# Small one-hots for the lists, row tiles in groups of four, and adj.T blocks gathered beside the scan: a change to a sparse two-layer graph kernel

## The chip, the core and the metric

The kernel runs on one core of a Trainium2 chip. The metric is the device time of one execution in microseconds (us); a kernel's time is the median of its timed runs. A ratio is always that of a kernel to the kernel before, measured on the same chip in the same rounds: the mean time of its runs over the mean of the other's. It is therefore not quite the ratio of the medians that I quote. Brackets after a ratio are its 95% interval.

Profiled times (starts of instructions, stages) come from one execution of each kernel.

## The reference, cut to what matters

Two layers, each preceded by a LayerNorm and a ReLU, and each with a residual. `x` is 4096 x 512, `adj` is 4096 x 4096 and sparse, with denser rows and columns at low indices.

```python
h = jnp.maximum(_layernorm(x), 0.0)
x = x + L0(h, adj, W)      # mx = h @ W, scaled by a tanh/artanh of norms;
                           # gamma from the row's square; A @ (gamma - 1), A @ (gamma * X), sum of A's rows;
                           # midpoint, relu, more tanh/artanh scalings
h = jnp.maximum(_layernorm(x), 0.0)
x = x + L1(h, adj, ...)    # node softmax(h @ node_w) * edge softmax where adj > 0, then adj * att @ (h @ weight)
```

## The kernel before

The kernel never multiplies by the whole of `adj`. For each of 32 row tiles (128 rows of `adj`) it finds which columns have any entry in that tile, packs them into a list, and gathers only those. Three stages matter.

**Stage A, for eight groups of four row tiles.** It loads adj.T in 64 pieces of 1 MB by the sync queue, reduces each piece to "which adj.T row has an entry in which row tile" (the scan), computes each entry's place in the list with small vector operations, and inverts that into a list by matmuls of one-hots (rows of zeros with a single one, which marks an entry's place). Beside it runs phase A: LayerNorm, `h @ W`, and the row `Y` with its extra columns, written to DRAM.

**Stage B.** For each row tile it gathers the listed blocks of adj.T (128 columns each, `at`) and the listed rows of Y (`yg`), multiplies them on TensorE, then does the midpoint and phase C (the projections of the second layer).

**Stage D.** Attention on gathered rows of `h`. The change leaves it alone.

```python
def gather_at(r):                       # adj.T blocks of one row tile
    n = CAPS[r]                         # 6 to 22, 256 in all
    wide = n > WIDE
    t = atp.tile([P, CAPM if wide else WIDE, P], F32, tag=f"at{wide}", bufs=2 if wide else 3)
    for k in range(n):
        nc.gpsimd.indirect_dma_start(out=t[:, k, :], in_=adj_rows, ...)
    nc.sync.dma_start(at_dram[r], t[:, :n, :])      # kept for a later stage
    at_sb[r] = t

def scan_loads(g):
    for b in range(NT // SC):
        s = ap.tile([P, SC, T4 * P], F32, tag="scan", bufs=3)
        nc.sync.dma_start(s, adj_t[...])             # the same sync queue
...
def make_list(r, lo, hi):
    nc.vector.tensor_tensor(oh, lo[:, q, :].unsqueeze(2).to_broadcast([P, NT, P]),
                            iota_h..., ALU.is_equal)  # 4096 elements a partition
    ...                                              # ov: 32 x n, compare and multiply
    for c in range(NT):
        nc.tensor.matmul(ps[:, :n], oh[:, c, :], ov[:, c, :], ...)
...
for g in range(NG):                                  # stage A
    a = [phase_a(2 * g), phase_a(2 * g + 1)]         # two row tiles each
    ...
    for r in range(g * T4, min(g * T4 + T4, AHEAD)): # AHEAD = 3: only the first three tiles
        gather_at(r)
...
for t in range(T4):                                  # stage B
    if r + AHEAD < NT:
        gather_at(r + AHEAD)
    acc = products(r)                                # gathers Y rows, multiplies with at_sb[r]
```

Of the kernel before, what the change touches and what calls it, by code (L numbers as in the profile page):

```python
# [27 lines left out]
F32 = mybir.dt.float32  # L28
F16 = mybir.dt.float16
# [9 lines left out]
P = 128  # L39
# [83 lines left out]
def listed_path(ctx, tc, x, adj_t, w0, weight, bias, node_w, edge_w, out, flag):  # L123
# [11 lines left out]
    YW = D + 2  # L135
    HALF = D // 2
# [18 lines left out]
    iota_i = const.tile([P, P], I32, tag="iotai", name="iotai")  # L155
    nc.gpsimd.iota(iota_i, [[1, P]], base=0, channel_multiplier=0)
    iota_h = const.tile([P, P], F16, tag="iotah", name="iotah")
    nc.vector.tensor_copy(iota_h, iota_i)
# [3 lines left out]
    nc.vector.tensor_copy(part_f, part_i)  # L162
    above_b = const.tile([P, P], BF16, tag="aboveb", name="aboveb")
    nc.vector.tensor_scalar(above_b, iota_h, part_f, None, ALU.is_gt)
# [6 lines left out]
    col_i = const.tile([P, NT], I32, tag="coli", name="coli")  # L171
    nc.gpsimd.iota(col_i, [[P, NT]], base=-(N // 2), channel_multiplier=1)
    col_h = const.tile([P, NT], F16, tag="colh", name="colh")
    nc.vector.tensor_copy(col_h, col_i)

# [4 lines left out]
    count = const.tile([P, NT], F32, tag="count", name="count")  # L180
    idx_y = const.tile([P, sum(CAPS)], I32, tag="idxy", name="idxy")
# [12 lines left out]
    atp = early.enter_context(tc.tile_pool(name="atp", bufs=1))  # L194
# [14 lines left out]
    def layernorm(pool, tag, xs, T, bufs):  # L209

        st = small.tile([P, T, nc.vector.BN_STATS_DIM], F32, tag=f"st{T}", name="st")
        mv = small.tile([P, T, nc.vector.BN_AGGR_DIM], F32, tag=f"mv{T}", name="mv")
        for t in range(T):
            nc.vector.bn_stats(st[:, t, :], xs[:, t, :])
            nc.vector.bn_aggr(mv[:, t, :], st[:, t, :])
        ve = S.tile("ve", T)
        nc.vector.tensor_scalar(ve, mv[:, :, 1], LN_EPS, None, ALU.add)
        rstd = S.recip(S.sqrt(ve, T), T, "rstd")
        z = pool.tile([P, T, D], F32, tag=tag, name="z", bufs=bufs)
        for t in range(T):  # L220
            nc.vector.tensor_scalar(  # L221
                z[:, t, :], xs[:, t, :], mv[:, t, 0:1], rstd[:, t : t + 1], ALU.subtract, ALU.mult
            )
        return z

    def relu_transposed(pool, z, T, bufs):

        hT = pool.tile([P, DC, T * P], F32, tag="hT", name="hT", bufs=bufs)
        for c in range(DC):
            tp = bank("tp", 2)  # L230
            for t in range(T):
                nc.tensor.transpose(tp[:, t * P : (t + 1) * P], z[:, t, c * P : (c + 1) * P], ident)  # L232
            nc.scalar.activation(hT[:, c, :], tp[:, : T * P], AF.Relu)
        return hT

    at_sb = {}

    def gather_at(r):

        n = CAPS[r]  # L240
        wide = n > WIDE
        t = atp.tile([P, CAPM if wide else WIDE, P], F32, tag=f"at{wide}", name="at", bufs=2 if wide else 3)
        for k in range(n):
            nc.gpsimd.indirect_dma_start(  # L244
                out=t[:, k, :],
                out_offset=None,
                in_=adj_rows,
                in_offset=bass.IndirectOffsetOnAxis(ap=idx_a[:, first[r] + k : first[r] + k + 1], axis=0),
            )
        nc.sync.dma_start(at_dram[r], t[:, :n, :])  # L250
        at_sb[r] = t

    AHEAD = 3


    with tc.tile_pool(name="a", bufs=1) as ap:

# [35 lines left out]
        def places(g, f, ps):  # L293
# [21 lines left out]
            nc.vector.tensor_scalar(lo_i, pos, P - 1, None, ALU.bitwise_and)  # L315
            hi_i = ap.tile(shape, I32, tag="hii", name="hii", bufs=2)
            nc.vector.tensor_scalar(hi_i, pos, 7, None, ALU.logical_shift_right)
# [6 lines left out]
        def make_list(r, lo, hi):  # L324

            n, q = CAPS[r], r % T4
            oh = ap.tile([P, NT, P], F16, tag="oh", name="oh", bufs=1)
            shape = [P, NT, P]
            nc.vector.tensor_tensor(  # L329
                oh,  # L330
                lo[:, q, :].unsqueeze(2).to_broadcast(shape),
                iota_h.unsqueeze(1).to_broadcast(shape),
                ALU.is_equal,
            )
            ov = ap.tile([P, NT, CAPM], F16, tag="ov", name="ov", bufs=2)
            shape = [P, NT, n]
            ov = ov[:, :, :n]
            nc.vector.tensor_tensor(
                ov,
                hi[:, q, :].unsqueeze(2).to_broadcast(shape),  # L340
                iota_h[:, :n].unsqueeze(1).to_broadcast(shape),
                ALU.is_equal,
            )
            nc.vector.tensor_mul(ov, ov, col_h.unsqueeze(2).to_broadcast(shape))
            ps = bank("sm", 2)
            for c in range(NT):
                nc.tensor.matmul(ps[:, :n], oh[:, c, :], ov[:, c, :], start=(c == 0), stop=(c == NT - 1))  # L347
            iy = idx_y[:, first[r] : first[r] + n]
            nc.vector.tensor_scalar(iy, ps[:, :n], float(N // 2), None, ALU.add)
            nc.vector.tensor_scalar(  # L350
                idx_a[:, first[r] : first[r] + n], ps[:, :n], float(NT), float(N // 2 * NT + r), ALU.mult, ALU.add
            )

        def phase_a(g):
            xs = x_sb[g * T2 // T4][:, g * T2 % T4 : g * T2 % T4 + T2, :]
            z = layernorm(ap, "z", xs, T2, 1)
            hss = S.tile("hss", T2)
            for t in range(T2):
                junk = ap.tile([P, D], F32, tag="junk", name="junk", bufs=2)
                nc.vector.scalar_tensor_tensor(  # L360
                    junk, z[:, t, :], 0.0, z[:, t, :], ALU.max, ALU.mult, accum_out=hss[:, t : t + 1]
                )
            hT = relu_transposed(ap, z, T2, 2)
            yield
            mss = S.tile("mss", T2)
            Y = ap.tile([P, T2, YW], F32, tag="Y", name="Y", bufs=2)
            ym = [bank("mm", 4) for _ in range(T2)]
            for t in range(T2):
                for c in range(DC):
                    nc.tensor.matmul(  # L370
                        ym[t], hT[:, c, t * P : (t + 1) * P], w0_sb[:, c, :], start=(c == 0), stop=(c == DC - 1)
                    )
                junk = ap.tile([P, D], F32, tag="junk", name="junk", bufs=2)
                nc.scalar.activation(junk, ym[t], AF.Square, accum_out=mss[:, t : t + 1])
            yield
            xn = S.norm(hss, T2)
            at = S.artanh_clipped(xn, T2)
            mn = S.norm(mss, T2)
            arg = S.mul(S.mul(mn, S.recip(xn, T2), T2), at, T2, "arg")
            th = S.tanh(arg, T2)  # L380
            s = S.mul(th, S.recip(mn, T2), T2, "s")
            alive = S.tile("alive", T2)
            nc.vector.tensor_scalar(alive, mss, EPS * EPS, None, ALU.is_gt)
            s = S.mul(s, alive, T2, "sl")

            xss = S.mul(S.mul(mss, s, T2), s, T2)
            gam = S.tile("gam", T2)
            nc.vector.tensor_scalar(gam, xss, -1.0, 1.0, ALU.mult, ALU.add)
            nc.vector.reciprocal(gam, gam)
            gm = S.tile("gm", T2)  # L390
            nc.vector.tensor_scalar(gm, gam, 2.0, 1e-15, ALU.mult, ALU.max)
            sg = S.mul(s, gm, T2, "sg")
            nc.vector.tensor_scalar(Y[:, :, HALF], gm, -1.0, None, ALU.add)
            nc.gpsimd.memset(Y[:, :, YW - 1], 1.0)  # L394
            for t in range(T2):
                nc.scalar.activation(Y[:, t, 0:HALF], ym[t][:, 0:HALF], AF.Copy, scale=sg[:, t : t + 1])
                nc.scalar.activation(Y[:, t, HALF + 1 : D + 1], ym[t][:, HALF:D], AF.Copy, scale=sg[:, t : t + 1])  # L397
            nc.scalar.dma_start(y_dram[g * T2 * P : (g + 1) * T2 * P, :].rearrange("(t p) d -> p t d", p=P), Y)
            yield

        for g in range(NG):
            a = [phase_a(2 * g), phase_a(2 * g + 1)]
            tiles = scan_loads(g)
            next(a[0])
            next(a[1])
            f, ps = scan_flags(g, tiles)
            next(a[0])
            next(a[1])
            lo, hi = places(g, f, ps)
            for q in range(T4):  # L410
                make_list(g * T4 + q, lo, hi)
                if q % 2:
                    next(a[q // 2])
            for r in range(g * T4, min(g * T4 + T4, AHEAD)):
                gather_at(r)
# [16 lines left out]
    def products(r):  # L432

        n = CAPS[r]
        acc = [bank("mm", 4) for _ in range(2)]
        for k in range(n):
# [7 lines left out]
            for h in range(2):  # L444
                nc.tensor.matmul(  # L445
                    acc[h][:, 0 : HALF + 1],
                    at_sb[r][:, k, :],
# [4 lines left out]
        at_sb.pop(r)  # L452
# [58 lines left out]
    def phase_c(g):  # L511
        z = layernorm(bp, "zt", x_sb[g], T4, 3)
        for t in range(T4):
# [3 lines left out]
                junk, z[:, t, :], 0.0, nw, ALU.max, ALU.mult, accum_out=logit[:, r : r + 1]  # L517
            )
        yield
        hT = relu_transposed(bp, z, T4, 1)  # L520
# [30 lines left out]
    for g in range(NG):  # L551
        tm = bp.tile([P, T4, D], F32, tag="zt", name="tm", bufs=3)
        da = small.tile([P, T4, 2], F32, tag="da", name="da")
        for t in range(T4):
            r = g * T4 + t
            if r + AHEAD < NT:
                gather_at(r + AHEAD)
# [653 lines left out]
```

## Time and profile before

The time before was 1924.02 us, the median of 3 runs (1923.54 to 1924.39).

I mark the stages by three starts that any profile shows: the first gather of a Y row (end of A), the first gather of an h row (end of B), and the end of the span. The first profile of this kernel was taken of an execution longer than the timed runs.

| profile of the kernel before | A, to the first Y gather | B, to the first h gather | rest | span |
|---|---|---|---|---|
| first | 545.9 | 748.6 | 705.7 | 2000.2 |
| taken again | 528.3 | 679.8 | 714.2 | 1922.3 |

These are two groups of the first profile. The columns are line, engine, operation, output and inputs, count; busy us in all and mean ns of one; idle time of the engine just before them, with what ended most of it.

```profile
L244 POOL DMA_INDIRECT at<-in_adj_t_dram,idxa x256 | 271.1, 1059 | 180.9 <-DVE idxa L350 92.5
L438 POOL DMA_INDIRECT yg<-y,idxy x256 | 249.4, 974 | 210.0 <-PE mm L445 97.2
```

The reader should see that GpSimd issues 512 gathers for A and B at about 1 us each. Its long idle time is no loss where something else is the bound: before the adj.T gathers 92.5 us of it are waits for lists, and before the Y gathers 97.2 are waits for TensorE to free a buffer.

### The profile page before, as it was taken

The numbers are of one execution on the slowest core, as the hardware profiler recorded it, in microseconds if no ns is written. First come the engines' busy times: TensorE is split into PE (matmuls) and PEld (weight loads), VectorE is DVE, ScalarE is ACT, GpSimd is POOL, SyncE is SP. The second block draws the span as 40 slices with busy tenths as digits, with TensorE's granted clock in tenths as the row PEclk, the third lists the DMA queues.
The fourth block names the chain that finished last, engine by engine and source line by source line (L and its number), as shares of the span: only waits on it lengthen the run. The fifth ranks groups of instructions, "written<-read, shape, count | busy, mean of one in ns | idle before, by whom it ended". The sixth has DMA issues, their size and how long they took to land. (4 is left out here: it accounts for less than half of the span.)

```text
span 2000.2 us, 18396 instructions
## 1 busy us (share of the span) xinstructions
PE 1383.7 (69%) x5872; PEld 804.4 (40%) x5872; DVE 851.8 (43%) x2794; ACT 521.9 (26%) x1053; POOL 805.6 (40%) x828
## 2 busy tenths in 40 slices
PE   0422444433385468776787898679999999998988
PEld 0211222221153245443454554345555455555554
DVE  5836999999700325242433455212122222222222
ACT  0211333323200213131331434123232232222222
POOL 0375000000066766675756661144444344444330
PEclk9766766655698679887887999889999999999999
DMA  9564555544265566664656663386887787777761
GB/s 364 169 152 128 187 190 189 188 150 145 80 191 158 134 176 180 186 194 125 206 158 189 199 189 139 116 324 230 277 271 258 267 270 287 252 255 270 260 234 55
DMA packets 146361, 399.56 MB, mean 200 GB/s; under 512 B 17488, under 2 KB 17488, under 8 KB 146000
## 3 DMA queue, kind: packets, MB, share of 16 engines
q0 software_dynamic: 65536, 218.42, 36.2%
q1 hardware_dynamic: 70416, 159.66, 22.1%
q10 hardware_dynamic: 10304, 20.22, 2.8%
q8 instruction: 49, 0.80, 0.2%
q14 instruction: 56, 0.46, 0.1%
HBM read 331.09 MB, written 67.14 MB: 199 GB/s over the span
## 5 line engine op out<-in xcount | busy, mean ns | idle before, releaser
L607 POOL DMA_INDIRECT h<-h,idxy x256 | 241.0, 942 | 345.6 <-PE sm L684 236.0
L445 PE MATMUL mm<-yg,at 128*128 128x257 f32 x1024 | 283.1, 429 | 129.1 <-DMA yg<-y,idxy 97.3
L244 POOL DMA_INDIRECT at<-in_adj_t_dram,idxa x256 | 271.1, 1059 | 180.9 <-DVE idxa L350 92.5
L438 POOL DMA_INDIRECT yg<-y,idxy x256 | 249.4, 974 | 210.0 <-PE mm L445 97.2
L445 PEld LDWEIGHTS mm<-yg,at 128*128 128x128 f32 x1024 | 207.1, 211 | 197.3 <-DMA yg<-y,idxy 133.2
L684 PE MATMUL sm<-h,wT 128*128 128x512 f32 x512 | 270.0, 629 | 6.1 <-DVE zt L699 4.9
L527 PE MATMUL mm<-w,hT 128*128 128x512 f32 x512 | 242.9, 625 | 28.5 <-issue 22.2
L619 ACT COPY kT<-tp 128x512 f32<-128x512 f32 x256 | 144.8, 582 | 367.5 <-PE tp L618 343.0
L634 PE MATMUL mm<-kT,q 128*128 128x512 f32 (+3 forms) x608 | 237.2, 532 | 3.6 <-ACT kT L619 2.0
L641 DVE TENSOR_SCALAR_CACHE_REDUCE e<-mm 128x512 f32<-128x512 f32 (+2 forms) x76 | 45.9, 606 | 319.9 <-PE mm L638 307.0
L275 DVE TENSOR_REDUCE mx<-scan 128x16 f32<-128x2048 f32 x64 | 145.7, 2279 | 63.2 <-issue 33.8
L618 PE MATMUL tp<-ident,h 128*128 128x128 f32 x1024 | 151.8, 279 | 22.9 <-DMA h<-h,idxy 20.7
L618 PEld LDWEIGHTS tp<-ident,h 128*128 128x128 f32 x1024 | 123.3, 143 | 98.7 <-issue 85.8
L527 PEld LDWEIGHTS mm<-w,hT 128*128 128x128 f32 x512 | 100.1, 201 | 144.4 <-issue 133.8
L347 PE MATMUL sm<-ov,oh 128*128 128x6 f16 (+8 forms) x1024 | 32.3, 169 | 174.3 <-DVE oh L329 110.9
L634 PEld LDWEIGHTS mm<-kT,q 128*128 128x128 f32 x608 | 110.2, 191 | 101.3 <-issue 77.6
L370 PE MATMUL mm<-w,hT 128*128 128x512 f32 x256 | 135.0, 676 | 9.9 <-ACT Y L397 9.9
L329 DVE TENSOR_TENSOR oh<-lo,iotah 128x4096 f16<-128x4096 f16 x32 | 141.3, 4417 | 0.0
L232 PE MATMUL tp<-ident,z 128*128 128x128 f32 x256 | 54.5, 352 | 103.3 <-DVE z L221 67.9
L394 POOL MEMSET Y<- 128x2 f32 x16 | 1.7, 106 | 294.3 <-DMA y<-Y 135.6
L561 DVE COPY da<-mm 128x1 f32<-128x1 f32 x64 | 9.7, 156 | 257.9 <-ACT tm L560 181.8
L684 PEld LDWEIGHTS sm<-h,wT 128*128 128x128 f32 x512 | 84.3, 196 | 48.8 <-issue 31.9
(164 smaller groups left out, 1382.4 us busy)
## 6 DMA issues: line engine op xcount, KB each, us to landing
scan<-in_adj_t_dram SPq DMA_DIRECT2D x64, 1024.0 KB
h<-h SPq DMA_DIRECT2D x32, 512.0 KB
y<-Y ACTq DMA_DIRECT2D x16, 514.0 KB
x<-in_x_dram ACTq DMA_DIRECT2D x8, 1024.0 KB
x<-x SPq DMA_DIRECT2D x8, 1024.0 KB
hhT<-hhT SPq DMA_DIRECT2D x32, 256.0 KB
q<-hhT SPq DMA_DIRECT2D x32, 256.0 KB
x<-x SPq DMA_DIRECT2D x32, 256.0 KB
```

The source lines that it names most:

```text
L244: nc.gpsimd.indirect_dma_start(out=t[:, k, :], out_offset=None, in_=adj_rows, in_offset=bass.IndirectOffsetOnAxis(ap=idx_a[:, first[r] + k ...
L275: nc.vector.tensor_reduce(mx[:, :, b * SC : (b + 1) * SC].rearrange("p r c -> p c r"), s.rearrange("p c (r i) -> p c r i", i=P), AX.X, ALU ...
L329: nc.vector.tensor_tensor(oh, lo[:, q, :].unsqueeze(2).to_broadcast(shape), iota_h.unsqueeze(1).to_broadcast(shape), ALU.is_equal,)
L370: nc.tensor.matmul(ym[t], hT[:, c, t * P : (t + 1) * P], w0_sb[:, c, :], start=(c == 0), stop=(c == DC - 1))
L438: nc.gpsimd.indirect_dma_start(out=y, out_offset=None, in_=y_dram, in_offset=bass.IndirectOffsetOnAxis(ap=idx_y[:, first[r] + k : first[r] ...
L445: nc.tensor.matmul(acc[h][:, 0 : HALF + 1], at_sb[r][:, k, :], y[:, h * (HALF + 1) : (h + 1) * (HALF + 1)], start=(k == 0), stop=(k == n - 1),
L527: nc.tensor.matmul(ps, hT[:, c, t * P : (t + 1) * P], w[:, c, :], start=(c == 0), stop=(c == DC - 1))
L607: nc.gpsimd.indirect_dma_start(out=h, out_offset=None, in_=h_dram, in_offset=bass.IndirectOffsetOnAxis(ap=idx_y[:, first[r] + k : first[r] ...
L618: nc.tensor.transpose(tp[:, c * P : (c + 1) * P], h[:, c * P : (c + 1) * P], ident)
L619: nc.scalar.copy(s["kT"][k // KG][:, :, k % KG * P : (k % KG + 1) * P], tp.rearrange("p (c j) -> p c j", c=DC))
L634: nc.tensor.matmul(ps[:, :w], s["q"][:, c * P : (c + 1) * P], kT[:, c, :w], start=(c == 0), stop=False)
L684: nc.tensor.matmul(s["acc"], s["w"][:, k % KG * P : (k % KG + 1) * P], s["h"].pop(k)[:, D : 2 * D], start=(k == 0), stop=(k == n - 1),)
```

## The change

Its intent has three parts.

(a) **Small one-hots.** A place in the list is split at 32 instead of 128 (`QB = 32`), so `oh` has 1024 elements a partition in place of 4096, laid out with NT innermost. `ov` becomes four times as wide. All lists of a group share one PSUM bank and are read out together.

(b) **Groups of four.** Phase A works on four row tiles at a time, and LayerNorm's output, ReLU and the sum of squares move from VectorE to ScalarE.

(c) **Early gathers.** All 256 adj.T blocks are gathered in stage A, beside the scan, stored in DRAM, and read back in stage B by plain DMAs of the sync queue.

```diff
-        oh = ap.tile([P, NT, P], F16, tag="oh", name="oh", bufs=1)
-        nc.vector.tensor_tensor(oh, lo[:, q, :].unsqueeze(2).to_broadcast(shape),
-                                iota_h.unsqueeze(1).to_broadcast(shape), ALU.is_equal)
+        oh = ap.tile([P, QB, NT], F16, tag="oh", name="oh", bufs=2)
+        nc.vector.tensor_tensor(oh, lo[:, j, :].unsqueeze(1).to_broadcast([P, QB, NT]), lo_of, ALU.is_equal)
   ... (ov, the matmuls and the read-out likewise, one PSUM bank for four lists)
-        z = layernorm(ap, "z", xs, T2, 1)
+        h = relu_layernorm(ap, "z", x_sb[g], T4, 1)          # ReLU and scaling on ScalarE
-                nc.vector.scalar_tensor_tensor(junk, z[:, t, :], 0.0, z[:, t, :], ALU.max, ALU.mult, accum_out=...)
+                nc.scalar.activation(junk, h[:, t, :], AF.Square, accum_out=hss[:, t : t + 1])
   ...
 def gather_at(r):
-    t = atp.tile([P, CAPM if wide else WIDE, P], F32, tag=f"at{wide}", name="at", bufs=2 if wide else 3)
+    t = ap.tile([P, CAPM if wide else WIDE, P], F32, tag=f"at{wide}", name="at", bufs=1 if wide else 3)
     for k in range(n):
         nc.gpsimd.indirect_dma_start(...)
     nc.sync.dma_start(at_dram[r], t[:, :n, :])
-    at_sb[r] = t
   ...
-            for r in range(g * T4, min(g * T4 + T4, AHEAD)):
+            for r in range(g * T4, g * T4 + T4):
                 gather_at(r)
   ...
 def products(r):
+    at = bp.tile([P, CAPM if wide else WIDE, P], F32, tag=f"at{wide}", name="at", bufs=1 if wide else 3)
+    nc.sync.dma_start(at[:, :n, :], at_dram[r])
   ...
-            if r + AHEAD < NT:
-                gather_at(r + AHEAD)
             acc = products(r)
```

In the new kernel the adj.T gathers are line 257, their stores line 263, the scan loads line 269, the scan's reduces line 282, the one-hots lines 339 to 345, the list matmuls line 348, the index writes line 357, the Y gathers line 443 and the products line 450.

## The prediction

> **What bounds the kernel now.** I read the engine tenths over the span first, then the groups of instructions, then the windows of the stage that the diff edits, then the waits and the timeline inside it. One proviso: the profiled execution spans 2000.2 us, the timed median is 1924.02, so my us are profiled ones, some 4% long.
>
> The engine tenths (40 slices of 50 us) show three stages.
>
> ```profile
> PE   0422444433385468776787898679999999998988
> ...
> DVE  5836999999700325242433455212122222222222
> ...
> POOL 0375000000066766675756661144444344444330
> ```
>
> The digits say that from 100 to 545 us (stage A: scan of adj.T, lists, first matmul, Y) VectorE is full while GpSimd is idle; from 545 to 1290 (stage B: weighted sums and phase C) GpSimd is at six or seven tenths and TensorE at seven or eight; after 1290 (stage D, attention) TensorE is full. The diff leaves D alone.
>
> Windows of equal kind in stage A (columns: window, its length, then busy us with counts of PE, PEld, DVE, ACT, POOL, then granted clock, DMA share, GB/s):
>
> ```profile
> 287.00:343.00 56.00, 23.38 (x178) 12.73 (x178) 54.03 (x149) 17.65 (x41) 0.20 (x2) 0.63 0.50 176
> 343.00:400.00 57.00, 22.53 (x178) 12.47 (x178) 54.96 (x152) 19.02 (x41) 0.20 (x2) 0.67 0.48 166
> ```
>
> One group of four row tiles takes about 56 us, of which VectorE works 54 to 55. The groups of instructions say on what:
>
> ```profile
> L275 DVE TENSOR_REDUCE mx<-scan 128x16 f32<-128x2048 f32 x64 | 145.7, 2279 | 63.2 <-issue 33.8 <-DMA scan<-in_adj_t_dram 29.2
> ...
> L329 DVE TENSOR_TENSOR oh<-lo,iotah 128x4096 f16<-128x4096 f16 x32 | 141.3, 4417 | 0.0
> ```
>
> The scan costs as much as the one-hots. Also real: the 33.8 us idle, at 113 to 147 us. The sync queue's timeline shows the stores of gathered blocks at 121 and the next scan loads only at 140.6, so loads stood behind stores that waited for gathers.
>
> In stage B one GpSimd instruction goes out every 1.25 us (0.94 us and 0.30 us before it) over long stretches:
>
> ```profile
> 892.98 0.94 POOL L244 DMA_INDIRECT at<-in_adj_t_dram,idxa  x1 [0.30 <-issue]
> 894.23 0.95 POOL L244 DMA_INDIRECT at<-in_adj_t_dram,idxa  x1 [0.30 <-issue]
> 895.48 0.94 POOL L244 DMA_INDIRECT at<-in_adj_t_dram,idxa  x1 [0.30 <-issue]
> 896.72 0.95 POOL L438 DMA_INDIRECT yg<-y,idxy  x1 [0.30 <-issue]
> ```
>
> Gathers of adj.T blocks and of Y rows share that one issuer, and the waits of TensorE in the groups name the Y rows (L445: 97.3 us in all). GpSimd issue and TensorE in turn bound B.
>
> **What the Trainium skill says.** "VectorE: DVE Perf Modes", section "The perf-mode tier table": 16-bit tensor_tensor in SBUF can run at 2 results a cycle, fp32 at one. "Vector Engine (DVE) Microarchitecture Reference", section "5.1 Performance modes": that needs an innermost step of 1 on every operand. The old one-hot reads `lo` with an innermost broadcast: 4417 ns for 4096 elements, with a fixed 150 ns, is 1.04 ns an element, one a cycle; the trace agrees. The new layout has NT innermost everywhere, so I expect two; no instruction of the trace before shows that. "SBUF — State Buffer", section "Practical consequences": GpSimd and some VectorE instructions exclude each other on a shared port, and tensor_reduce never contends. The trace agrees in part: an adj.T gather beside a one-hot lasted 5.05 us in place of 0.94, beside reduces 0.94; the page says tensor_tensor contends with reads only, the trace shows it holding up a gather.
>
> **The change part by part.** Back-to-back VectorE instructions start about 0.07 us apart beyond their streaming time (timeline), so I cost each as elements plus 0.07.
>
> VectorE in A, in all:
> - One-hot `oh`: 4096 to 1024 elements. Was 32 x 4.34 = 139 us. At two a cycle 0.53 + 0.07 = 0.60, x32 = 19. Saves 120.
> - `ov`, compare and multiply: elements rise four-fold, from 32 x 256 to 32,768 a pass. Was 2 x (8.5 + 2.2) = 21; becomes 2 x (17.1 + 2.2) = 39. Costs 18.
> - LayerNorm output and sum of squares to ScalarE: 18 + 23 saved; ScalarE gets 32 x (0.6 + 0.8) = 45 us, minus half its small instructions and table loads. At 18 us of 56 it has room.
> - Groups of four row tiles: the instruction order shows VectorE at 1207 instructions before the first sum, 814 after; some 330 of the 393 gone are tiny, x 0.07 = 23 saved.
> Sum: 441 busy before (windows 0 to 546), minus 120, plus 18, minus 41, minus 23 = 275. That is 34 us a group.
>
> So VectorE stops being A's bound. GpSimd now gathers all 256 blocks in A: 256 x 1.25 = 320 us, and it can't start before the first list, at about 78 us as before (79 us now). That gives 398 us. Additions: VectorE holding the port (short instructions now, say 0.05 us a gather, 13), memsets of Y in GpSimd's order, waits for buffers (one wide, three narrow), stores and scan loads in one sync queue (the built order has scan loads alternating with stores that wait for gathers). I take 35 us for all. A's last gather at about 433, first product at 445; it was 548 (GpSimd's first Y gather at 545.9). Gain 100.
>
> DMA in that stretch: 16.8 MB gathered and 16.8 MB stored move beside 56 MB of scan. From 78 to 113 us gathers alone took 0.31 of the DMA time for about 27 gathers, so 0.4 us of all engines each, 102 in all; the other 87 MB at the 364 GB/s of the first slice take 240. 342 of some 360 us: nearly full, which is why I don't take the 398.
>
> Stage B: 208 adj.T gathers x 1.25 = 260 us leave GpSimd, which keeps 256 x 1.25 = 320. The blocks come back by the sync queue (16.8 MB more read). With operands at hand seven blocks took 6.25 us on TensorE, 0.89 each; sixteen matmuls of phase C took 7.03. Until 622 us no adj.T gather ran, so group 0 (59 blocks at 1.43, the rate with eight Y buffers) stays 84 us. Middle: 197 x 0.89 = 175, plus 384 x 0.44 = 169, plus transposes 40 = 384, plus some 60 of waits on ScalarE that the trace has now ("issue" and "remote" rows). Tail as now, 77. Sum 605 against 742 (548 to 1290): 137, of which I count 115, because TensorE may not fill so well.
>
> Total: 100 + 115 = 215 profiled, about 200 in timed runs. 1924 - 200 = 1724; I say 1725.
>
> **Rivals.**
> 1. DMA or the sync queue becomes A's bound. For it: 342 us of DMA work above; the 33.8 us wait, once before, can now recur for each group; where gathers and scan overlapped (147 to 172 us) VectorE worked only 9.17 of 25 us. Against: the scheduler lets scan loads run over a group ahead. Then A gains 20 to 40 and the time is about 1790.
> 2. B doesn't speed up, since Y gathers (eight in flight, 1.43 us each at 184 GB/s) and ScalarE's slow stretches pace it. For it: from 700 to 1200 TensorE waited only 45 us for Y rows, some 60 for others. Against: GpSimd's unbroken stretches. Then B gains 50: about 1790.
> 3. `ov` and `oh` run at one a cycle. VectorE then needs 275 + 17 + 34 = 326 us, 41 a group, about GpSimd's pace: costs 10 to 20 us.
> 4. More than expected: without gaps TensorE's granted clock (0.84 in mid-B, 1.00 in D) rises and B takes 540: about 1660.
>
> **Range and chances.** Rivals 1 and 2 together give about 1850, rival 4 about 1650. Range 1640 to 1815. To miss 2% both gains must fail, for which only rival 1 at its worst, starving VectorE in every group, is a way: faster 0.94, same 0.04, slower 0.02.
>
> **What would show it.** Right: `oh` near 0.68 us and no GpSimd idle in A; its last adj.T gather near 430 us; first Y gather near 440; no adj.T gather in B; TensorE in mid-B over 0.85 busy; D still about 700 us. Wrong: VectorE idle waiting for scan loads, sync-queue stores waiting for gathers, gathers well over 1 us, or a first product after 490; in B, TensorE waiting as long for Y rows as before, or for reloaded blocks.

## The result, and the profile after

The changed kernel took 1820.95 us (median of 4, 1818.66 to 1821.51) against 1923.88 (1923.54 to 1924.39): ratio 0.9463 [0.9446, 0.9479]. It is faster by 103 us. I had said 1725, with a range of 1640 to 1815: the direction was right, the gain was half of what I had summed, and the time lies just outside the range.

The engine tenths of the kernel after (40 slices of 45 us each):

```profile
PE   0671534555717879999999975899999998898988
...
DVE  5863476556400236444564530122222222222222
...
POOL 1067653355666755445443204344444443344330
```

Stage A is the first twelve digits. VectorE is no longer full there, which is what (a) and (b) were for. But nothing else is full either: GpSimd, which should have become the bound, runs at three to seven tenths. From slice 13 on (stage B) TensorE is at seven to nine, up to the passage to stage D (slices 24 and 25).

The end of A is the first start in the view of the Y gathers (count; shortest, median and longest in ns; first and last start):

```profile
L443 POOL DMA_INDIRECT yg<-y,idxy x256: 940/946/1408, 531.6 to 1010.7; - x128
```

The groups of instructions, after:

```profile
L257 POOL DMA_INDIRECT at<-in_adj_t_dram,idxa x256 | 248.6, 971 | 266.1 <-DVE ml L113 91.0
L443 POOL DMA_INDIRECT yg<-y,idxy x256 | 252.9, 988 | 234.1 <-PE mm L450 178.4
L450 PE MATMUL mm<-yg,at 128*128 128x257 f32 x1024 | 246.9, 394 | 74.1 <-DMA yg<-y,idxy 65.6
...
L282 DVE TENSOR_REDUCE mx<-scan 128x16 f32<-128x2048 f32 x64 | 145.9, 2281 | 112.6 <-DMA scan<-in_adj_t_dram 112.6
```

In B, GpSimd now mostly waits for TensorE to free a Y buffer (178.4 us, against 97.2 in the first profile of before and 40.8 in the second), and TensorE's wait for Y rows is 65.6 us (97.3 and 113.7 before): the stage has passed to TensorE. In A, VectorE waited 112.6 us for scan tiles, against 63.2 us of idle time before those reduces in the first profile of before, and 70.4 in the second. GpSimd was idle 266.1 us before the adj.T gathers; 91.0 of these are the wait for the first list.

What holds up the scan loads stands in the waits of the sync queue in stage A (0 to 500 us; columns: waiting line, what it waited for, us in all, times, longest):

```profile
SPq L263 <- DMA at<-in_adj_t_dram,idxa: 274.7, 71, 22.1
```

The queue spent 274.7 us waiting for gathers to land, so that it could start their stores; 214.0 of these fell before its last scan load went out at 433 us, and only they can hold up loads. Its timeline, in one group's stretch (start, length, what was issued):

```profile
213.84 0.32 SPq L263 DMA_DIRECT2D at<-at  x1
214.27 0.38 SPq L269 DMA_DIRECT2D scan<-in_adj_t_dram  x1
224.65 0.32 SPq L263 DMA_DIRECT2D at<-at  x1
225.08 22.88 SPq L269 DMA_DIRECT2D scan<-in_adj_t_dram  x7
```

Here one scan load goes out right behind each store, and the stores come about 11 us apart (213.84 and 224.65, and one before at 202.25), which is the time of nine gathers, one row tile. With the group's last store gone at 224.65, seven loads follow within 23 us, with no store between them. VectorE's timeline over the same stretch shows what that does to the scan (the bracket is idle time before the instruction and what ended it):

```profile
222.31 2.29 DVE L282 TENSOR_REDUCE mx<-scan 128x16 f32<-128x2048 f32 x1 [8.45 <-DMA scan<-in_adj_t_dram]
...
241.74 0.19 DVE L357 SCALAR_TENSOR_TENSOR idxa<-idxy,tileof 128x32 int32<-128x32 int32 x1
```

VectorE stood idle for 8.45 us before that tile (and for 7.97 and 3.76 us before the ones beside it), and the group's index write came only at 241.74. GpSimd's timeline shows the circle close:

```profile
221.06 0.94 POOL L257 DMA_INDIRECT at<-in_adj_t_dram,idxa  x1 [0.30 <-issue]
222.00 0.12 POOL L400 MEMSET Y<- 128x1 f32 x1
242.20 0.94 POOL L257 DMA_INDIRECT at<-in_adj_t_dram,idxa  x1 [20.08 <-DVE rstd L118]
```

GpSimd ran out of lists at 222.12 us. The next list's indices were written at 241.74, and its gathers began 20 us late, at 242.20. (The releaser that the row names, `rstd`, is another VectorE instruction; releasers are inferred, and it is the index write that ends at 241.93, just before.) This happened five times in A: 22.6, 20.1, 22.8, 22.3 and 13.2 us, 101.0 us together.

Where the time went, by stage, in profiled us:

| | A | B | rest | span |
|---|---|---|---|---|
| before, taken again | 528.3 | 679.8 | 714.2 | 1922.3 |
| after | 531.6 | 567.0 | 718.3 | 1816.9 |
| gain | -3.3 | 112.8 | -4.1 | 105.4 |

The whole gain lies in B. A, in which I had counted on 100 us, gained nothing.

### The profile page after: what moved, and what is told of

Same layout as the page of the kernel before. It is cut to its first block, busy times and chain, and to the rows that moved or that the text cites. A ratio compares the mean times of both kernels' runs of the same rounds, so it can differ in the third digit from the quotient of the medians. Undisturbed runs are those within 1.5% of the kernel's fastest.

```text
span 1816.9 us, 18260 instructions
## 1 busy us (share of the span) xinstructions
PE 1375.9 (76%) x5872; PEld 827.6 (46%) x5872; DVE 689.1 (38%) x2345; ACT 560.0 (31%) x1092; POOL 793.2 (44%) x878
## 5 line engine op out<-in xcount | busy, mean ns | idle before, releaser
L257 POOL DMA_INDIRECT at<-in_adj_t_dram,idxa x256 | 248.6, 971 | 266.1 <-DVE ml L113 91.0
L443 POOL DMA_INDIRECT yg<-y,idxy x256 | 252.9, 988 | 234.1 <-PE mm L450 178.4
L450 PE MATMUL mm<-yg,at 128*128 128x257 f32 x1024 | 246.9, 394 | 74.1 <-DMA yg<-y,idxy 65.6
L450 PEld LDWEIGHTS mm<-yg,at 128*128 128x128 f32 x1024 | 193.9, 195 | 121.5 <-issue 51.2
L531 PE MATMUL mm<-w,hT 128*128 128x512 f32 x512 | 227.9, 596 | 0.0
L282 DVE TENSOR_REDUCE mx<-scan 128x16 f32<-128x2048 f32 x64 | 145.9, 2281 | 112.6 <-DMA scan<-in_adj_t_dram 112.6
L232 PE MATMUL tp<-ident,h 128*128 128x128 f32 x256 | 60.7, 370 | 157.6 <-ACT h L221 135.1
L620 PE MATMUL tp<-ident,h 128*128 128x128 f32 x1024 | 153.7, 281 | 21.8 <-DVE mask L632 14.4
L620 PEld LDWEIGHTS tp<-ident,h 128*128 128x128 f32 x1024 | 125.0, 145 | 97.9 <-issue 86.2
L531 PEld LDWEIGHTS mm<-w,hT 128*128 128x128 f32 x512 | 95.6, 191 | 104.1 <-issue 100.0
L374 PE MATMUL mm<-w,hT 128*128 128x512 f32 x256 | 128.0, 656 | 8.5 <-ACT Y L402 5.0
L232 PEld LDWEIGHTS tp<-ident,h 128*128 128x128 f32 x256 | 38.7, 185 | 187.9 <-ACT h L221 136.9
L348 PE MATMUL sm<-ov,oh 128*32 128x24 f16 (+8 forms) x1024 | 68.6, 230 | 59.9 <-DVE ov L345 59.9
L348 PEld LDWEIGHTS <-oh 128*32 128x32 f16 x1024 | 66.7, 146 | 66.6 <-DVE oh L339 45.8
L663 ACT ACTIVATE e<-e,rmax 128x512 f32<-128x512 f32 (+2 forms) x76 | 49.5, 652 | 146.9 <-DVE rmax L658 146.9
```

The source lines that it names most:

```text
L257: nc.gpsimd.indirect_dma_start(out=t[:, k, :], out_offset=None, in_=adj_rows, in_offset=bass.IndirectOffsetOnAxis(ap=idx_a[:, first[r] + k ...
L282: nc.vector.tensor_reduce(mx[:, :, b * SC : (b + 1) * SC].rearrange("p r c -> p c r"), s.rearrange("p c (r i) -> p c r i", i=P), AX.X, ALU ...
L348: nc.tensor.matmul(ps[:QB, o : o + m], oh[:, :, c], ov[:, :, c], start=(c == 0), stop=(c == NT - 1))
L374: nc.tensor.matmul(ym[t], hT[:, c, t * P : (t + 1) * P], w0_sb[:, c, :], start=(c == 0), stop=(c == DC - 1))
L443: nc.gpsimd.indirect_dma_start(out=y, out_offset=None, in_=y_dram, in_offset=bass.IndirectOffsetOnAxis(ap=idx_y[:, first[r] + k : first[r] ...
L450: nc.tensor.matmul(acc[h][:, 0 : HALF + 1], at[:, k, :], y[:, h * (HALF + 1) : (h + 1) * (HALF + 1)], start=(k == 0), stop=(k == n - 1),)
```

## The experiments

My theory: the stores of gathered blocks wait, in the sync queue, for gathers; scan loads stand behind them; so the lists come late; so the gathers come late, which delays the next stores. The rival that I took most seriously: the DMA engines are full in A, with up to 33.6 MB more moved beside the scan (16.8 gathered and 16.8 stored), and the order in a queue is a symptom. Others: ScalarE or the small steps of phase A hold VectorE up, or my figure for A before was wrong because its profile was of a long execution. Each expectation names the theories that it tells apart.

The changed kernel was not run again beside the experiments. Where I say that a run is so many us faster than the change, I compare medians of different rounds, and the kernel before itself had medians from 1920.16 to 1926.96 us in them. By the ratios, times 1924, the gains over the change are 15 us for gather_late, 36 for store_pool, 60 for store_no_wait, 15 for memset_dve, 58 for store_pool_memset and 64 for store_lag_memset: a few us apart from those of the medians, and the same in kind.

### before_again: the kernel before, unchanged

No edit. It asks whether the 2000.2 us of the first profile belong to the kernel.

> The kernel before, unchanged, profiled a second time: the trace that the prediction rests on spans 2000.2 us although the timed median is 1924. Theory 1 (that one profiled execution lost some 76 us in stage B, in the rows named issue and remote): span near 1924, first Y gather still near 546 us, first h gather of stage D near 1220 instead of 1294. Theory 2 (every profiled execution of this kernel is long): span near 2000 again.

It took 1924.14 us (one look), with a span of 1922.3. The view of its Y gathers gives the end of A:

```profile
L438 POOL DMA_INDIRECT yg<-y,idxy x256: 940/946/1456, 528.3 to 1120.0; - x128
```

So the first profile was of one long execution, by 78 us: 17.6 more in A, 68.8 more in B, 8.5 less in the rest. Everything that the prediction reads from B of the first profile is inflated by that. What made that one execution long stays open.

### gather_late: parts (a) and (b) alone

Based on the kernel after, with the gathers put back into B. Some buffers had to become single for the room (the scan's small tiles, `junk`, and two `Y` instead of three).

```diff
-            for r in range(g * T4, g * T4 + T4):
+            for r in range(g * T4, min(g * T4 + T4, AHEAD)):
                 gather_at(r)
   ...
-        nc.sync.dma_start(at[:, :n, :], at_dram[r])
-                    at[:, k, :],
+                    at_sb[r][:, k, :],
   ...
+            if r + AHEAD < NT:
+                gather_at(r + AHEAD)
             acc = products(r)
```

> The changed kernel with its third part undone: adj.T blocks are gathered in stage B three tiles ahead and used from SBUF, as before; small one-hots and groups of four stay (a few small stage-A buffers single, to fit). Theory 1 (stores that wait for gathers hold up the scan loads in the sync queue, and that alone kept stage A long): without them VectorE paces A at 35 to 42 us a group, first Y gather at 400 to 430 us, B as in the kernel before, time 1790 to 1830. Theory 2 (A is held by the lists, the DMA rate of the scan or the groups of four themselves): first Y gather at 500 or later, time 1880 to 1920.

It took 1806.73 us (1802.08 to 1814.79), ratio 0.9384 [0.9347, 0.9421]. That is faster than the whole change. This is the Y gather's row by its source line (count; shortest, median and longest in ns; first and last start):

```profile
L447 POOL DMA_INDIRECT yg<-y,idxy x256: 942/949/1412, 410.0 to 998.4; - x128
```

A ends at 410.0, so (a) and (b) gain 118 us there, and B is as long as before (678.9). Put on top of them, part (c) takes 112 us out of B and adds 122 to A: it costs 14 us in the timed runs (1807 to 1821).

### gather_early_alone: part (c) alone

Based on the kernel before.

```diff
-        t = atp.tile([P, CAPM if wide else WIDE, P], F32, tag=f"at{wide}", name="at", bufs=2 if wide else 3)
+            t = ap.tile([P, CAPM if wide else WIDE, P], F32, tag=f"at{wide}", name="at", bufs=1 if wide else 3)
   ...
-            for r in range(g * T4, min(g * T4 + T4, AHEAD)):
+            for r in range(g * T4, g * T4 + T4):
                 gather_at(r)
   ... (products reloads at_dram[r] as in the change)
```

> The kernel before with the third part alone: all adj.T blocks gathered in stage A, stored, read back in B; one-hots and groups of two as before. Theory 1 (stage B gains because GpSimd is relieved; stores delay the scan a little, since VectorE at 56 us a group is slower than the gathers): first Y gather at 550 to 590 us, stage B as short as in the changed kernel (567 us from first Y gather to first h gather), time 1830 to 1870. Theory 2 (B's gain comes from the other two parts): B as long as before, time 1930 to 1960.

It took 1983.08 us (1978.32 to 1987.27), ratio 1.0301 [1.0269, 1.0332]: slower than before by 3%. B was as short as expected (568.1 us), but A grew to 699.3 us, 109 beyond the upper end of what I had expected; this is the largest miss. The two longest waits of all engines up to 700 us (the first row includes 76.8 us until the first list):

```profile
POOL at L243 <- DVE idxa L344: 283.1, 7, 76.8
DVE mx L269 <- DMA scan<-in_adj_t_dram: 215.5, 22, 33.6
```

It is the same circle, stronger; the sync queue's own view has 505.9 us of waiting for gathers before stores. Gathers started at 78.9 us and would need 256 x 1.25 = 320 us; the last one began at 692.2. Of the 613 us between, 206.3 (283.1 - 76.8) are six waits for lists. A second cost lies beside the circle: the gathers were busy 331.3 us in place of some 242 (256 x 0.945), because 25 of them lasted 4.03 to 5.05 us. Each of the 25 started while one of the long one-hots (4.42 us) ran, and ended 0.8 to 1.0 us after it; with the small one-hots of the change no gather lasted over 1.44 us. VectorE waits 215.5 us for scan tiles and then still has the long one-hots to do before a list is ready, so I take each turn of the circle to be longer than with (a) and (b), which no run shows by itself. I had added the costs of the stages instead of going round.

### onehot_alone: part (a) alone

Based on the kernel before, with `make_lists` of the change, the old phase A in groups of two, and the gathers in B. The small tiles of the scan and `junk` are single for the room.

```diff
-            oh = ap.tile([P, NT, P], F16, tag="oh", name="oh", bufs=1)
+                oh = ap.tile([P, QB, NT], F16, tag="oh", name="oh", bufs=1)
   ... (the rest of make_lists as in the change)
-            for q in range(T4):
-                make_list(g * T4 + q, lo, hi)
-                if q % 2:
-                    next(a[q // 2])
+            make_lists(g, lo, hi)
+            next(a[0])
+            next(a[1])
```

> The kernel before with the small one-hots alone. VectorE in A falls from 441 to some 339 us by the prediction's sum, 43 us a group. Theory 1 (VectorE paces A when few stores stand in the sync queue): first Y gather at 440 to 470, time 1830 to 1860. Theory 2 (something other than VectorE paces A): time over 1890.

It took 1859.4 us (1851.35 to 1868.78), ratio 0.9662 [0.9616, 0.9708], with A ending at 456.7, both as expected. Part (a) is thus worth 72 us of A, and part (b) on top of it another 47 (456.7 to 410.0). It also shows a small cost of (a): its first adj.T gather started at 92.6 us, before's at 78.3, because no index is written before all four lists of a group are through the matmuls: the first index write came at 91.06 us, right behind the fourth list's last matmul, and in the kernel before at 77.75, behind the first list's. (A single `oh` buffer made VectorE wait 5.5 us more there.)

### store_pool: the stores issued by GpSimd

Based on the kernel after. Only the issuer of the stores changes; GpSimd issues each store behind the gathers of its row tile.

```diff
-            nc.sync.dma_start(at_dram[r], t[:, :n, :])
+            return t[:, :n, :]
   ...
-                gather_at(r)
+                t = gather_at(r)
+                nc.gpsimd.dma_start(at_dram[r], t)
```

> The changed kernel with one edit: the stores of gathered blocks are issued by GpSimd in place of the sync queue, which then holds scan loads alone in stage A. Theory 1 (stores in the sync queue hold up the scan loads): VectorE's wait for scan tiles falls from 112.6 us to under 50, the last adj.T gather moves from 523 to about 440 to 470 us, time 1740 to 1780. Theory 2 (the DMA rings are full, so the queue's order doesn't matter): VectorE waits as long as in the changed kernel, time within 1% of 1821.

It took 1782.79 us (1778.21 to 1787.81), ratio 0.9278 [0.9223, 0.9333]: 38 us less than the change, with the same bytes moved, and 3 us over the upper end of what I had expected. The sync queue's timeline shows no store among the loads any more:

```profile
61.19 223.27 SPq L269 DMA_DIRECT2D scan<-in_adj_t_dram  x32
```

From the waits of all engines up to 500 us:

```profile
DVE Y L399 <- DMA y<-Y: 64.8, 6, 30.1
...
DVE mx L282 <- DMA scan<-in_adj_t_dram: 28.2, 16, 7.3
...
POOL at L418 <- DMA at<-in_adj_t_dram,idxa: 23.0, 11, 5.2
...
POOL at L257 <- DVE f L290: 13.9, 1, 13.9
```

The wait for scan tiles fell from 112.6 to 28.2 us, and the waits for lists from 101.0 to 13.9. The gathers' time now adds up: 256 gathers of 0.991 us with 0.30 before each are 330, lists 13.9, waits before stores 28.7 (23.0 for gathers), and 32 stores of 0.58 us are 18.5; that makes 391, and the gathers ran from 97.7 to 488.0, that is 390. The last gather was later than I had expected (440 to 470), since the stores themselves cost GpSimd 47 us there. The longest row of VectorE's waits is now that for a free Y buffer, which the next edits leave. "Within 1% of 1821" is excluded.

### store_act: the stores issued by ScalarE

As store_pool, with `nc.scalar.dma_start(at_dram[r], t)`.

> The same edit with ScalarE's queue as the issuer of the stores. Theory 1: scan loads flow as in the run with GpSimd, but ScalarE now waits for gathers between its own instructions, so phase A's chain (Relu, squares, Y) is late: time between 1750 and 1821. Theory 2 (rings full): within 1% of 1821 or slower.

It took 1830.86 us (1825.9 to 1838.02), ratio 0.953 [0.9471, 0.9589]: no gain over the change, outside the range that my theory gave. By its time alone it is what the rival forecast ("within 1% of 1821 or slower"); the waits have to decide. VectorE's wait for scan tiles did fall, to 24.3 us. The waits of all engines up to 500 us have in its place:

```profile
ACT junk L378 <- DMA at<-in_adj_t_dram,idxa: 67.4, 7, 16.4
...
POOL at L257 <- DVE idxa L357: 62.6, 4, 23.9
...
DVE nm L73 <- ACT junk L378: 42.2, 4, 15.6
```

ScalarE's own instructions now stood behind stores that waited for gathers: 173.7 us in six rows of that view, of which the longest is shown. GpSimd again waited for lists, four times. VectorE needs ScalarE's sums of squares before it goes on with phase A, and by that way the lists came late again. The circle is the same with another engine in it. So it is not the sync queue that matters, but that the waiting store shares an in-order issuer with something that the lists need.

### store_no_wait: the same bytes stored, but waiting for nothing

Its output is wrong, which doesn't matter for the time. The sync queue stores as many bytes as the change does, but from a weight tile that was loaded long ago, so no store waits for a gather.

```diff
-            nc.sync.dma_start(at_dram[r], t[:, :n, :])
+            ready = weight_sb.rearrange("p c (k i) -> p (c k) i", i=P)
+            for o in range(0, n, 16):
+                m = min(16, n - o)
+                nc.sync.dma_start(at_dram[r][:, o : o + m, :], ready[:, :m, :])
```

> Wrong result on purpose: the changed kernel, whose stores of adj.T blocks in the sync queue take their bytes from a weight tile that is long loaded, so the same bytes are stored by the same queue but no store waits for a gather; the gathers run and their data are dropped. Theory 1 (it is the wait for gathers in the sync queue that starves the scan): the first Y gather comes at 440 to 490 us and the time is 1740 to 1780. Theory 2 (the stores' bytes beside scan and gathers fill the DMA engines): as the changed kernel, first Y gather over 515 us, time within 1% of 1821.

It took 1766.55 us (1762.54 to 1770.64), ratio 0.9152 [0.9121, 0.9184], with A ending at 481.8:

```profile
L446 POOL DMA_INDIRECT yg<-y,idxy x256: 943/949/1405, 481.8 to 968.7; - x128
```

The stores' bytes are still there, in the same queue and beside the same gathers; the wait is gone, and with it 54 us. GpSimd's waits for lists fell from 101.0 to about 45 us. So it was not the load of the DMA engines that held A at 531.6. (Gathers also need not wait here for a store to free their buffer; but that wait was only 0.6 us in the change.)

### memset_dve: the last column of Y set by VectorE

Based on the kernel after. Up to 450 us ScalarE had waited 32.5 us (4 times, up to 16.1) for GpSimd's memset of Y, which stands in GpSimd's order behind gathers that wait for lists.

```diff
-                nc.gpsimd.memset(Y[:, YW - 1 : YW], 1.0)
+                nc.vector.memset(Y[:, YW - 1 : YW], 1.0)
```

> The changed kernel with one edit: the memset of Y's last column on VectorE in place of GpSimd, where it stood in order behind gathers (ScalarE waited 32.5 us for it and VectorE 27.7 for Y buffers). Theory 1 (stores in the sync queue are the main hold): a gain of 0 to 20 us, 1800 to 1821. Theory 3 (the memsets behind gathers are the main hold): a gain of 40 us or more.

It took 1807.85 us (1805.84 to 1815.62), ratio 0.9387 [0.935, 0.9423]: a gain of 13 us, whose interval is clear of the change's. A ended at 520.2 in place of 531.6, and GpSimd's waits for lists fell from 101.0 to 92.5 us. I read the memset as a second, smaller path of the same circle.

### store_pool_memset: both edits

```diff
-                nc.gpsimd.memset(Y[:, YW - 1 : YW], 1.0)
+                nc.vector.memset(Y[:, YW - 1 : YW], 1.0)
   ...
-                gather_at(r)
+                t = gather_at(r)
+                nc.gpsimd.dma_start(at_dram[r], t)
```

> Both edits: stores issued by GpSimd, the memset of Y on VectorE. With stores gone from the sync queue, VectorE still waited 59.6 us for Y buffers. If the memsets behind gathers are what remains: first Y gather at 465 to 485 us (GpSimd's own 98 + 320 + stores of 40 or so), time 1755 to 1775. If not: as the run with the stores alone, 1783.

It took 1766.96 us (1766.62 to 1767.71), ratio 0.9162 [0.9133, 0.9191], so the two edits roughly add up (38 and 13, and 54 together). A ended at 487.5, just over the 485 that I had allowed. The last scan tile was reduced at 347.2 us, in place of 441.4 in the change, while the last adj.T gather started at 479.9. The scan runs well ahead of the gathers, and after the first list no wait for a list is left: from there on GpSimd alone bounds A.

### store_lag_memset: the store of a row tile issued behind the gathers of the next

GpSimd still waits where it issues a store just behind the last gather of the tile. Here the store is held back by one tile, which the three narrow buffers allow.

```diff
             for r in range(g * T4, g * T4 + T4):
-                gather_at(r)
+                if held and CAPS[r] > WIDE:
+                    put(*held.pop())
+                t = gather_at(r)
+                if held:
+                    put(*held.pop())
+                held.append((r, t))
   ... (put issues nc.gpsimd.dma_start; the memset on VectorE as above)
```

> As the run before, and each narrow tile's store is issued one tile later, so that GpSimd needn't wait for its own gathers to land (23 us of waits in the run with stores on GpSimd). If these waits lie on the path: 10 to 25 us less than the run before; if they are hidden by waits for lists: the same.

It took 1761.77 us (1757.98 to 1764.9), ratio 0.9133 [0.91, 0.9166]. It is the fastest kernel, and beats the kernel before and the change. Over store_pool_memset it gains 5 us where I had expected 10 to 25, and the intervals of their ratios overlap, so this last step is not shown, though in the same rounds all four of its runs lie below all four of the other's. A ends 11.6 us earlier (475.9). The gathers ran from 98.8 to 467.9, 369 us; waits before stores are still 24.6 us of that, and the stores themselves 18.6.

## Why the prediction was wrong, point by point

**The step that failed** is the term "Additions" of stage A: "memsets of Y in GpSimd's order, waits for buffers (one wide, three narrow), stores and scan loads in one sync queue (...). I take 35 us for all." Counted from the first list, that term measured 105 us: gathers ran from 98.2 to 523.5 us, 425 in place of the 320 of pure pace; 101.0 of the difference are the five waits for lists; the other 4 are small (gathers lasted 971 ns in the mean and not 945, and memsets of Y stand between them). A further 20 us came from the step before it: I had put the first list at "about 78 us as before", and it came at 98.2. Of these 20, onehot_alone shows about 14 to belong to reading all lists of a group together. So A's last gather came at 523.5 and not at 433, and the gain of 100 was -3.

The term was not only mis-sized; it was treated in the wrong way. I listed the parts of a circle as costs to be added up, after I had quoted the wait (33.8 us) and named it in rival 1 as one that "can now recur for each group". What I set against it, that the scheduler lets scan loads run over a group ahead, did not hold: once the stores began, the loads of a group mostly stood behind them until its last store was gone. Rival 1 is what happened, in its queue half: store_no_wait and store_pool show that it was the wait and not the DMA work. It was worse than I had let it be: I gave A "20 to 40" in that case and it gained nothing.

**The sum for VectorE nearly held.** In A it was busy 440.7 us in the first profile of before and 290.2 after, 150 less; the terms of the prediction make 166 (120 - 18 + 41 + 23), which would leave 275. In onehot_alone it was busy 340.5 us in A, where the terms of (a) leave 339; so what is missing lies in part (b). The one-hot, from the view of its source line:

```profile
L339 DVE TENSOR_TENSOR oh<-lo,loof x32: 661/684/694, 69.0 to 471.5; 128x1024 f16<-128x1024 f16 x32
```

684 ns for 1024 elements is two a cycle by the prediction's own reckoning (0.53 streaming and 0.15 fixed): rival 3 fell. The Trainium skill agrees: in "VectorE: DVE Perf Modes", section "The perf-mode tier table", a 16-bit tensor_tensor in SBUF reaches two results a cycle. The old one-hot, with its innermost broadcast, took 4417 ns for 4096 elements. Parts (a) and (b) alone took 118 us out of A, more than I had counted for A with all three.

**GpSimd's pace held.** One gather every 1.25 us while lists were at hand; the mean gather in A lasted 971 ns and the longest 1437, so the port that it shares with VectorE did not hold it up for long, as assumed (0.05 us a gather). That is owed to part (a), as gather_early_alone shows.

**The DMA estimate was too high as a bound.** I had counted 342 us of DMA work in A and called it nearly full. One reading in it was wrong: from 78 to 113 us 19 gathers started, not 27, and GpSimd's queue moved 1.10 MB (17 blocks) in 27% of the engines' time, so a gather would cost some 0.56 us of all engines and the sum would be 383, still further off. In store_lag_memset, the DMA share over the 371 us from the first gather to the last was 0.79, which makes 293 us of work, and in store_pool_memset the scan was over at 347 us, 133 before the last gather.

**Stage B held.** I counted 115 us and measured 112.8; gather_early_alone, with (c) alone, measured the same 112. That the number fits so well is partly luck. The prediction's sum for B, 605 us, was 38 too high (567), the 742 that it was set against was 62 too high (680 in the second profile), and of the 137 between them I had kept 115 by judgement. Also, 187 adj.T gathers left B, not 208, since 69 had already gone out in A. Rival 2 fell. Windows of B, of the kernel before (profile taken again) and of the change, starting 4 us apart in absolute time and alike in their place in B (columns: window, length, busy us and counts of PE, PEld, DVE, ACT, POOL, then granted clock, DMA share, GB/s):

```profile
528.00:700.00 172.00, 109.53 (x371) 73.22 (x372) 28.97 (x130) 21.45 (x38) 125.62 (x131) 0.80 0.64 178
700.00:900.00 200.00, 170.30 (x555) 105.84 (x555) 79.05 (x341) 60.12 (x104) 143.25 (x147) 0.90 0.66 200
```

```profile
532.00:704.00 172.00, 135.45 (x501) 95.52 (x502) 45.60 (x216) 40.14 (x68) 106.64 (x111) 0.90 0.74 235
704.00:904.00 200.00, 191.34 (x715) 123.79 (x714) 98.55 (x411) 89.24 (x152) 98.92 (x100) 1.00 0.70 237
```

TensorE did 501 matmuls in place of 371 in the first 172 us, and 715 in place of 555 in the next 200, where it is 96% busy. GpSimd, busy for 73 and 72% of these windows before, is busy for 62 and 49% now. The clock granted rose with it, from 0.80 and 0.90 to 0.90 and 1.00. That is the mechanism of rival 4; how much of the 113 us it makes, no run separates. The profiles give an estimate: over all of B, for the same 1792 matmuls, TensorE was busy 542.7 us before and 500.0 after, at a granted clock of 0.89 and 0.95. So some 43 us go with shorter matmuls, and 70 with less idle time.

**Stage D held**: 714.2 before, 718.3 after, as "still about 700".

**The chances.** I gave "faster" 0.94 and that was right. The range left no room for the failure of one gain: with A's gain gone and B's whole, the prediction's own numbers give 1924 - 115 x 0.96 = 1814, at the very edge of my 1815. Rivals 1 and 2, one at a time, had been put at 1790 because I granted A a part of its gain even where the circle closed.

## What to carry to other kernels

When a change makes a producer wait for a consumer's results in the same in-order queue that feeds the producer (here: store behind gather, gather behind list, list behind scan load, scan load behind store), go round the circle once before adding up costs; its price can be paid in every group (here in five of seven). Give a DMA that waits for late data an issuer that has nothing else urgent to do: here GpSimd, whose gathers are what the store waits for anyway, worked, and ScalarE, whose results the lists need, did not. And before trusting the length of a stage, compare the profiled execution with the timed runs: a span 4% over the median is a reason to look at a second profile.

## What the Trainium skill lacked or had wrong

- "DMA: Bandwidth & Descriptors", section "Issuing engines are not separate DMA queues", says that initiating DMAs on several engines "will only save the time on the sequencer it takes to initiate the DMA". That section leaves out DMAs that wait for a semaphore. The page's section "Anatomy of one DMA — SWDGE (gpsimd) path" does place such a wait on the issuing sequencer, but not even there is it said that the issuer's later DMAs then stand behind it. Here the sync queue waited 214.0 us before stores while it still had scan loads to issue, and another issuer for the same stores made the kernel 38 us faster (1821 to 1783), while a third one made it no faster (1831).
- "SBUF — State Buffer", section "Practical consequences", says that tensor_tensor with both inputs in SBUF contends with GpSimd's reads, and infers that descriptor generation, which needs the write side, goes free. It does not say on which side an indirect gather falls, which reads its indices from SBUF. In the kernel before, the first adj.T gathers, beside one-hots of 4.42 us, lasted 5.05, 4.29 and 4.14 us in place of 0.94 (starts at 78.31, 84.93 and 90.77 us of the profile taken again); in gather_early_alone 25 gathers lasted 4.03 to 5.05. With one-hots of 0.68 us the longest gather of A lasted 1.44 us.
- I found no page with the pace of indirect DMAs from GpSimd: one gather of 128 rows each 1.25 us here (0.94 busy and 0.30 before it), which bounds stage A in the best kernel.
- Nor did I find one that says that a profiled execution can be 78 us longer than the kernel's timed ones, with everything else equal. Its cause stays open.
